# A down product whose sixth chunk is contracted over all 128 rows

## The chip, the cores and the metric

The kernel runs on one NeuronCore of one Trainium2 chip. The metric is the device time of one execution in microseconds. Engines are named as in the profile: PE (TensorE matmuls), PEld (TensorE weight loads), DVE (VectorE), ACT (ScalarE), POOL (GpSimd), SP (SyncE, which issues the DMAs).

## The reference

The program is one transformer-like block on x of shape (4, 2048, 256) in fp32: two kinds of attention without a softmax, each followed by the same feed-forward network, all with a layer norm ahead and a residual sum behind.

```python
x = x + attn_a(layernorm(x))    # projections, exponentials, a weight per head
x = x + ffn(layernorm(x))
x = x + attn_b(layernorm(x))    # products over the 4 batch rows of a token, two gates
x = x + ffn(layernorm(x))

def fp4_linear(x, w):                       # both operands rounded blockwise to a 4-bit grid
    return einsum('bsk,nk->bsn', fp4(x), fp4(w))

def ffn(x):                                 # w_gate, w_up: (704, 256); w_down: (256, 704)
    h = silu(fp4_linear(x, w_gate)) * fp4_linear(x, w_up)
    return fp4_linear(h, w_down)            # the down product
```

`fp4` scales each block of 16 numbers by its largest magnitude and rounds to eight magnitudes. The inner width of 704 matters here: it is 5.5 times 128.

## The kernel before, in words

The 2048 token positions are cut into 16 groups of 128; a group holds the 4 batch rows of its positions, so it is 4 tiles of 128 tokens (`S = 4`, `NJ = 16`). Every group goes through attention a, the first network, attention b and the second network. In a network each of the 4 tiles goes through `ffn_tile`, so there are 16 × 4 × 2 = 128 calls.

One call of `ffn_tile` does this:

1. PE multiplies the tile by both halves of the gate and up weights, 352 columns each (L1190). ACT takes the silu (L1211), DVE multiplies (L1222).
2. DVE, ACT and POOL round the 704 columns to the grid (`quantize`: L340, L1024, L345, L351, L359, L360, L1051).
3. PE transposes the rounded tile in six chunks of 128 columns (L1245), and ACT copies them from PSUM into `hqT`, of shape 128 × 6 × 128 (L1257).
4. PE forms the down product: six matmuls that accumulate in one PSUM bank, chunk i of `hqT` against chunk i of the weights `wdT`, of shape 128 × 6 × 256 (L1270). All operands are fp32, and each matmul stands in the profile as two records.
5. DVE adds the result to the tokens (L301 or L1302).

The chunks start at the columns

```python
HC = [i * 128 for i in range(5)] + [FF - 128]      # 0, 128, 256, 384, 512, 576
```

The sixth starts at 576, not 640, so that it too is a whole 128 × 128 transpose. Its first 64 columns are those that the fifth chunk already covers. So in the kernel before, the sixth matmul uses only rows 64 to 127 of both operands:

```python
rows = slice(P // 2 if i == 5 else 0, P)
```

`wdT` is filled once, near the start: `w_down` is rounded in two pieces, transposed in the same six chunks (L683), and copied from PSUM by ACT in four pieces (L692), which carry the tokens `("wd", 0)` to `("wd", 3)`. Pieces 1 and 3 hold chunks 3 to 5.

The order of the work is not left to the engines. The class `Plan` collects all operations with an engine, an estimated duration, a rank, and the tokens that they read and write, and plays them through in a list scheduler: an engine that is free takes the ready operation with the lowest rank, under the limits of the buffers' pools. The instructions are then issued in that order, and each engine works through its own queue in order. Waits between engines follow from the tiles' contents. A down product has rank `at + 19` and the estimate 2.95 us there.

Of the kernel before, what the change touches and what calls it, by code (L numbers as in the profile page):

```python
# [17 lines left out]
P = 128  # L18
# [4 lines left out]
FF = 704  # L23
HF = FF // 2
FB = FF // BLK

HC = [i * 128 for i in range(5)] + [FF - 128]
LN_EPS = 1e-5
# [8 lines left out]
def blocks(ap, n=BLK):  # L37
    return ap.rearrange("p (g e) -> p g e", e=n)
# [16 lines left out]
class Plan:  # L55
# [23 lines left out]
    def op(self, engine, us, rank, fn, reads=(), writes=(), port=False, table=None, land=0.0, spare=None):  # L79


        i = len(self.ops)
        after = set()
        for t in reads:
            if t in self.last:
                after.add(self.last[t])
        for t in writes:
            after.update(self.readers.get(t, ()))
            if t in self.last:
                after.add(self.last[t])  # L90
        for t in reads:
            self.readers.setdefault(t, []).append(i)
        for t in writes:
            self.last[t] = i
            self.readers[t] = []
        bufs = list(dict.fromkeys(t[0] for t in (*reads, *writes) if isinstance(t[0], Buf)))
        for b in bufs:
            b.users += 1
        self.ops.append(
            dict(engine=engine, us=us, rank=rank, fn=fn, bufs=bufs, port=port, table=table,  # L100
                 land=land, spare=spare or {}, then=[], left=len(after), at=0.0)
        )
        for a in sorted(after):
            self.ops[a]["then"].append(i)
# [108 lines left out]
def kernel(  # L213
# [29 lines left out]
    nc = tc.nc  # L243
# [10 lines left out]
    def one(shape, name, pool=wp, dtype=F32):  # L254
        return pool.tile(shape, dtype, tag=name, name=name)
# [19 lines left out]
    wdT = one([P, 6, D], "wdT")  # L275
# [89 lines left out]
    def tiles(name, n, shape, pool, dtype=F32):  # L365
        made = [one(shape, f"{name}{i}", pool, dtype) for i in range(n)]
        plan.pool(name, made)
        return made
# [6 lines left out]
    floored = tiles("xn", 1, [P, S * D // BLK, BLK + 1], fp)  # L375
    floored += tiles("h", 3, [P, FB, BLK + 1], fp)
    tiles("qax", 2, [P, S * D], fp)
# [4 lines left out]
    tiles("qm", 2, [P, FF], fp, BF16)  # L382
    tiles("sh", 5, [P, 3, FB], fp)
    tiles("hqT", 2, [P, 6, P], fp)
# [14 lines left out]
    def first_pass():  # L399
        op = plan.op  # L400
# [164 lines left out]
        def quantize(at, load, p, n):  # L565
            raw, a, m, w = (plan.buf(t) for t in ("hqT", "qa", "qm", "sh"))
            g = n // BLK

            def ap(b):
                whole = b.ap if len(b.ap.shape) == 2 else b.ap.rearrange("p c n -> p (c n)")  # L570
                return whole[:p, :n]

            def sc(i):
                return w.ap[:p, i, :g]

            op("SP", 0.7, at - 8, lambda: load(ap(raw)), (), [(raw, 0)], land=3.0)
            op(
                "DVE",
                0.9 + n / 1000.0,
                at,  # L580
                lambda: scales(ap(raw), sc(0), sc(1), sc(2)),
                [(raw, 0)],
                [(w, 0)],
            )
            op(
                "DVE",
                0.15 + n / 1000.0,
                at + 1,
                lambda: over_scales(ap(a), blocks(ap(raw)), sc(2)),
                [(raw, 0), (w, 0)],  # L590
                [(a, 0)],
                port=True,
            )
            op(
                "ACT",
                0.2 + n / 1200.0,
                at + 2,
                lambda: to_steps(ap(m), ap(a)),
                [(a, 0)],
                [(m, 0)],  # L600
            )
            op(
                "DVE",
                0.3 + n / 500.0,
                at + 3,
                lambda: to_grid(ap(a), ap(a), ap(m)),
                [(m, 0)],
                [(a, 0)],
                port=True,
            )  # L610
            op(
                "POOL",
                0.2 + n / 550.0,
                at + 5,
                lambda: nc.gpsimd.tensor_mul(
                    blocks(ap(a)), blocks(ap(a)), over_blocks(sc(1))
                ),
                [(w, 0)],
                [(a, 0)],
                port=True,  # L620
            )
            return a
# [10 lines left out]
        for t, (w, wT) in enumerate(((w_gate, wgT), (w_up, wuT))):  # L633
            for i in range(4):
# [13 lines left out]
                def turn(a=a, tp=tp):  # L648
                    for c in range(KC):
                        for t in range(2):  # L650
                            nc.tensor.transpose(
                                tp.ap[:, (2 * c + t) * R : (2 * c + t + 1) * R],
                                a.ap[:R, t * D + c * P : t * D + (c + 1) * P],
                                ident[:R, :R],
                            )
# [13 lines left out]
        for i in range(2):  # L669
            at = 32.0 + 2.0 * i  # L670
            a = quantize(
                at,
                lambda dst, i=i: nc.sync.dma_start(dst, w_down[i * P : (i + 1) * P, :]),
                P,
                FF,
            )
            for h in range(2):
                tp = plan.buf("bank")

                def turn(a=a, tp=tp, h=h):  # L680
                    for c in range(3):
                        at = HC[3 * h + c]
                        nc.tensor.transpose(  # L683
                            tp.ap[:, c * P : (c + 1) * P], a.ap[:, at : at + P], ident
                        )

                op("PE", 0.5, at + 8, turn, [(a, 0)], [(tp, 0)])
                op(
                    "ACT",
                    0.45,  # L690
                    at + 9,
                    lambda tp=tp, h=h, i=i: nc.scalar.copy(  # L692
                        wdT[:, 3 * h : 3 * h + 3, i * P : (i + 1) * P],
                        tp.ap[:, : 3 * P].rearrange("p (c n) -> p c n", c=3),
                    ),
                    [(tp, 0)],
                    [("wd", 2 * i + h)],
                )


        op(
# [222 lines left out]
        op("DVE", 1.4, FIRST, join_biases, [(GROW, "m"), ("rn", 0)], [("ssq", 0), ("bvz z", 0), ("lb", 0)])  # L924

    first_pass()


# [4 lines left out]
    def group(j):  # L933
# [4 lines left out]
        def op(engine, us, at, fn, reads=(), writes=(), **kw):  # L938
            plan.op(engine, us, base + at, fn, reads, writes, **kw)
# [241 lines left out]
        def ffn_tile(at, k, s, xqT):  # L1181
            h, qa, qm, sh = (plan.buf(p) for p in ("h", "qa", "qm", "sh"))
            for half in range(2):
# [3 lines left out]
                def hidden(g=g, u=u, cols=cols):  # L1187
                    for bank, w in ((g, wgT), (u, wuT)):
# [33 lines left out]
                    lambda u=u, sil=sil, half=half: nc.vector.tensor_mul(  # L1222
                        h.ap[:, half * FB // 2 : (half + 1) * FB // 2, :BLK],
                        blocks(sil.ap),
# [14 lines left out]
            hqT = plan.buf("hqT")  # L1239
# [25 lines left out]

            def down():
                for i in range(6):

                    rows = slice(P // 2 if i == 5 else 0, P)
                    nc.tensor.matmul(  # L1270
                        o.ap[:, :D],
                        hqT.ap[rows, i, :],
                        wdT[rows, i, :],
                        start=(i == 0),
                        stop=(i == 5),
                    )
# [3 lines left out]
                2.95,  # L1280
                at + 19,
                down,
                [(hqT, 0), (hqT, 4)] + [("wd", i) for i in range(4)],
                [(o, 0)],
# [308 lines left out]
```

## Time and profile before

| | |
|---|---|
| median of 3 runs | 1665.7 us (1664.18 to 1666.67) |
| the profiled execution's own time | 1663.5 us |
| its span, from the first to the last instruction | 1661.7 us |
| mean granted clock of TensorE | 0.985 |
| PE busy | 1575.4 us (95%) |
| PEld busy | 1058.1 us (64%) |
| DVE busy | 1476.0 us (89%) |
| ACT busy | 808.0 us (49%) |
| POOL busy | 705.7 us (42%) |
| DMA | 27.68 MB, mean 17 GB/s |

A group in the profile stands by line, engine, operation and tiles: out<-in, the number of records, busy time and mean duration of one, then the idle time just before them and what ended it. A form like 64*128 64x256 is rows and columns of the weights in the array, then rows and columns of what streams through. PE records overlap: [...] a weight load can lie under the matmul ahead of it. The ends of matmuls are modelled, their starts are measured. "issue" is time in which the engine waited for nothing that the profile shows.

### The profile page before, as it was taken

To read this page: it belongs to the slowest core of one execution; us is meant where nothing else is said; L and a number is where in the kernel's file an instruction comes from. 1 tells how busy PE (TensorE), PEld (TensorE's weight loads), DVE (VectorE), ACT (ScalarE), POOL (GpSimd) and SP (SyncE) were. 2 spreads that over 40 slices of the span, in tenths; PEclk is the share of its full clock that TensorE was granted. 3 is DMA by queue.
4 is the path that set the end of the run, shared out by engine and by line. 5 is a ranking of instruction groups with operands and counts; after the bars stand their busy time and mean duration, and the time that the engine had idled before them with its cause. 6 is when DMAs were issued, how large, how long until landed. Compare 5 with 4: busy or idle time off the path is not lost.

```text
span 1661.7 us, 18801 instructions
## 1 busy us (share of the span) xinstructions
PE 1575.4 (95%) x6364; PEld 1058.1 (64%) x6364; DVE 1476.0 (89%) x2310; ACT 808.0 (49%) x1738; POOL 705.7 (42%) x739
## 2 busy tenths in 40 slices
PE   7888999999999999999999999999999999889798
PEld 6635656666666676666666666666666666556575
DVE  8988898999898989999997998989999888899874
ACT  5545456463544354545544564553744534353342
POOL 5334346434535343443543443344634424543531
PEclk9989999999999999999999999999999999999899
DMA  8200000000000000000000000000000000000000
GB/s 258 69 9 1 0 1 0 4 7 23 4 20 7 20 7 20 7 20 4 4 23 4 20 4 23 4 4 7 7 7 4 4 7 4 4 7 4 10 16 20
DMA packets 28872, 27.68 MB, mean 17 GB/s; under 512 B 3432, under 2 KB 28520, under 8 KB 28776
## 3 DMA queue, kind: packets, MB, share of 16 engines
q1 hardware_dynamic: 28776, 26.49, 5.1%
q8 instruction: 50, 0.82, 0.2%
q14 instruction: 46, 0.38, 0.1%
HBM read 18.09 MB, written 8.39 MB: 16 GB/s over the span
## 4 chain that ended last, share of the span: by engine, by line
PE 53%; DVE 33%; ACT 4%; POOL 4%; issue 4%; DMA 1%; POOLq 0%; SPq 0%; DVEq 0%; ACTq 0%
PE bank L1190 22%; PE bank L1270 14%; PE bank L981 11%; PE bank L1245 3%; DVE qa L345 3%; DVE qa L359 3%; DVE qa L360 3%; PE bank L958 2%; DVE tok L1497 2%; DVE h L1222 2%; DVE sh L340 2%; DVE pp L1496 2%; DVE x L301 1%; DVE sc L1382 1%; DVE qax L345 1%
## 5 line engine op out<-in xcount | busy, mean ns | idle before, releaser
L1051 POOL TENSOR_TENSOR qa<-qa,sh 128x704 f32<-128x704 f32 x128 | 193.1, 1510 | 461.3 <-DVE qa L360 361.0
L1270 PE MATMUL bank<-wdT,hqT 128*128 128x256 f32 (+1 forms) x1536 | 383.6, 393 | 4.6 <-ACT hqT L1257 3.9
L1190 PE MATMUL bank<-wgT,turned 128*128 128x352 f32 x1024 | 355.2, 470 | 17.0 <-DVE h L1222 12.7
L1190 PE MATMUL bank<-wuT,turned 128*128 128x352 f32 x1024 | 345.6, 460 | 0.4 <-DVE h L1222 0.4
L1270 PEld LDWEIGHTS bank<-wdT,hqT 128*128 128x128 f32 (+1 forms) x1536 | 277.5, 191 | 97.3 <-issue 48.9
L1190 PEld LDWEIGHTS bank<-wuT,turned 128*128 128x128 f32 x1024 | 195.3, 191 | 110.3 <-issue 1.9
L1190 PEld LDWEIGHTS bank<-wgT,turned 128*128 128x128 f32 x1024 | 183.8, 192 | 119.1 <-issue 26.0
L1211 ACT ACTIVATE sil<-bank 128x352 f32<-128x352 f32 x256 | 116.7, 459 | 167.3 <-PE bank L1190 120.5
L1222 DVE TENSOR_TENSOR h<-sil,bank 128x352 f32<-128x352 f32 x256 | 127.9, 508 | 53.8 <-PE bank L1190 46.7
L351 ACT ACTIVATE qm<-qa 128x704 bf16<-128x704 f32 (+1 forms) x138 | 107.6, 781 | 133.7 <-DVE qa L345 128.8
L1257 ACT COPY hqT<-bank 128x512 f32<-128x512 f32 (+1 forms) x256 | 111.0, 479 | 93.7 <-PE bank L1245 93.4
L359 DVE SCALAR_TENSOR_TENSOR qa<-qm,qa 128x704 f32<-128x704 bf16 (+1 forms) x138 | 129.5, 938 | 13.8 <-ACT qm L351 13.8
L360 DVE SCALAR_TENSOR_TENSOR qa<-qm,qa 128x704 f32<-128x704 bf16 (+1 forms) x138 | 137.2, 994 | 4.8
L1478 POOL TENSOR_TENSOR pp<-vg,sc 128x1024 f32<-128x1024 f32 x64 | 132.8, 2089 | 9.1 <-DVE fac L1415 6.0
L345 DVE SCALAR_TENSOR_TENSOR qa<-sh,h 128x704 f32<-128x704 f32 x128 | 131.4, 1031 | 1.9 <-PE bank L1245 0.6
L981 PE MATMUL bank<-wvz,turned 128*128 128x512 f32 x256 | 122.4, 616 | 5.7 <-DVE vz L1079 3.6
L981 PE MATMUL bank<-wqkB,turned 128*128 128x512 f32 x256 | 121.7, 598 | 3.0 <-ACT turned L965 2.6
L965 ACT COPY turned<-bank 128x512 f32<-128x512 f32 x160 | 87.8, 586 | 73.7 <-PE bank L958 72.5
L340 DVE TENSOR_REDUCE sh<-h 128x44 f32<-128x748 f32 x128 | 118.9, 929 | 3.3
L1245 PE MATMUL bank<-ident,qa 128*128 128x128 f32 x768 | 109.4, 278 | 12.3 <-POOL qa L1051 6.0
L1245 PEld LDWEIGHTS bank<-ident,qa 128*128 128x128 f32 x768 | 88.0, 141 | 46.9 <-issue 20.7
L1051 POOL TENSOR_TENSOR qax<-qax,sx 128x1024 f32<-128x1024 f32 x32 | 65.6, 2053 | 81.7 <-DVE qax L360 75.0
(171 smaller groups left out, 2318.2 us busy)
## 6 DMA issues: line engine op xcount, KB each, us to landing
x<-in_L_attn_a_x_dram SPq DMA_DIRECT2D x24, 512.0 KB, 5.1
out_dram<-x SPq DMA_DIRECT2D x64, 128.0 KB, 1.7
hqT<-in_L_ffn_w_gate_dram SPq DMA_DIRECT2D x4, 176.0 KB
hqT<-in_L_ffn_w_up_dram SPq DMA_DIRECT2D x4, 176.0 KB
hqT<-in_L_ffn_w_down_dram SPq DMA_DIRECT2D x2, 352.0 KB
pp<-in_L_attn_a_Wq_dram SPq DMA_DIRECT2D x2, 256.0 KB
pp<-in_L_attn_a_Wk_dram SPq DMA_DIRECT2D x2, 256.0 KB, 5.9
wvz<-in_L_attn_a_Wv_dram SPq DMA_DIRECT2D x1, 256.0 KB
```

What stands on the lines that cost most here:

```text
L340: nc.vector.tensor_reduce(amax, src, AX.X, ALU.max, apply_absolute_value=True)
L345: nc.vector.scalar_tensor_tensor(blocks(a), over_blocks(rs), -6.0 * BELOW, src, ALU.mult, ALU.mult)
L359: nc.vector.scalar_tensor_tensor(a, m, FLOOR, a, ALU.max, ALU.add)
L360: nc.vector.scalar_tensor_tensor(dst, m, FLOOR, a, ALU.max, ALU.subtract)
L981: nc.tensor.matmul(bank.ap[:, :n], lhs.ap[:, c, s * P : (s + 1) * P], w[:, c, :], start=(c == 0), stop=(c == KC - 1),)
L1051: lambda: nc.gpsimd.tensor_mul(blocks(a.ap), blocks(a.ap), over_blocks(q.ap[:, 1, :])),
L1190: nc.tensor.matmul(bank.ap[:, :HF], xqT.ap[:, c, s * P : (s + 1) * P], w[:, c, cols], start=(c == 0), stop=(c == KC - 1),)
L1211: lambda g=g, sil=sil: nc.scalar.activation(sil.ap, g.ap[:, :HF], AF.Silu),
L1222: lambda u=u, sil=sil, half=half: nc.vector.tensor_mul(h.ap[:, half * FB // 2 : (half + 1) * FB // 2, :BLK], blocks(sil.ap), blocks(u.ap[: ...
L1245: nc.tensor.transpose(bank.ap[:, (i - i0) * P : (i - i0 + 1) * P], qa.ap[:, HC[i] : HC[i] + P], ident,)
L1270: nc.tensor.matmul(o.ap[:, :D], hqT.ap[rows, i, :], wdT[rows, i, :], start=(i == 0), stop=(i == 5),)
L1478: nc.gpsimd.tensor_mul(pv.ap.rearrange("p t (n e) -> p t n e", e=HD), vg.ap[:, :, :D].rearrange("p t (n e) -> p t n e", e=HD), over_blocks ...
```

## The change

The sixth matmul takes all 128 rows of `hqT` and `wdT`, like the other five. So that the 64 columns that the fifth chunk covers are not counted twice, the first 64 rows of the sixth weight chunk are set to zero, once, by a memset on POOL. It writes over what ACT copied there and carries the tokens of pieces 1 and 3, so it comes after these two copies and before the first down product.

```diff
@@ after the copies of w_down into wdT
+        op(
+            "POOL",
+            0.3,
+            40.0,
+            lambda: nc.gpsimd.memset(wdT[: P // 2, 5, :], 0.0),
+            (),
+            [("wd", 1), ("wd", 3)],
+        )
@@ ffn_tile
             def down():
                 for i in range(6):
-
-                    rows = slice(P // 2 if i == 5 else 0, P)
                     nc.tensor.matmul(
                         o.ap[:, :D],
-                        hqT.ap[rows, i, :],
-                        wdT[rows, i, :],
+                        hqT.ap[:, i, :],
+                        wdT[:, i, :],
                         start=(i == 0),
                         stop=(i == 5),
                     )
```

The estimate of 2.95 us for the down product is left as it was. Lines of the kernel behind the insertion move by up to nine numbers (the down product from L1270 to L1277).

## Prediction

> **What bounds the kernel now.** I read the page's busy shares first, then the chain, then the PE groups by form, and last the PE timeline around one down product.
>
> ```profile
> PE 1575.4 (95%) x6364; PEld 1058.1 (64%) x6364; DVE 1476.0 (89%) x2310; ACT 808.0 (49%) x1738; POOL 705.7 (42%) x739
> PE   7888999999999999999999999999999999889798
> PEclk9989999999999999999999999999999999999899
> PE 53%; DVE 33%; ACT 4%; POOL 4%; issue 4%; DMA 1%; POOLq 0%; SPq 0%; DVEq 0%; ACTq 0%
> PE bank L1190 22%; PE bank L1270 14%; PE bank L981 11%; PE bank L1245 3%; DVE qa L345 3%; DVE qa L359 3%; DVE qa L360 3%; PE bank L958 2%; DVE tok L1497 2%; DVE h L1222 2%; DVE sh L340 2%; DVE pp L1496 2%; DVE x L301 1%; DVE sc L1382 1%; DVE qax L345 1%
> ```
>
> PE is nearly full from the fifth slice on, at a granted clock of almost 1. VectorE is close behind at 89%. The chain that ends last runs over PE for 53% of the span and over VectorE for 33%, so PE is the first bound but not the only one. The edited line, L1270, holds 14% of the span on that chain by itself.
>
> The groups by form split the down product into its five full chunks and its sixth (each fp32 product leaves two records, so 1280 + 256 records are 128 downs of six products):
>
> ```profile
> L1270 PE MATMUL bank<-wdT,hqT 128*128 128x256 f32 x1280 | 304.8, 386 | 4.6 <-ACT hqT L1257 3.9 <-DVE vz L1079 0.4 <-DVE x L1302 0.2
> L1270 PE MATMUL bank<-wdT,hqT 64*128 64x256 f32 x256 | 89.1, 428 | 0.0
> L1270 PEld LDWEIGHTS bank<-wdT,hqT 64*128 64x128 f32 x256 | 37.7, 184 | 42.8 <-issue 42.8
> ```
>
> Half the rows give a longer matmul record, 428 ns against 386, and 42.8 us of idle weight loader in front of the 64-row loads, for which no engine is named. These are not yet costs, since matmul records overlap and their ends are modelled. Starts are measured, so I take costs from the timeline (start, length, group), first around a down, then around another product of 256 columns with 128 rows throughout:
>
> ```profile
> 1599.09 1.35 PE L1190 MATMUL bank<-wuT,turned 128*128 128x352 f32 x4
> 1600.27 1.04 PE L958 MATMUL bank<-ident,qax 128*128 128x128 f32 x8
> 1601.14 2.95 PE L1270 MATMUL bank<-wdT,hqT 128*128 128x256 f32 x12
> 1604.02 1.45 PE L1190 MATMUL bank<-wgT,turned 128*128 128x352 f32 x4
> 1605.31 1.35 PE L1190 MATMUL bank<-wuT,turned 128*128 128x352 f32 x4
> ...
> 250.55 1.46 PE L981 MATMUL bank<-woB,turned 128*128 128x256 f32 x6
> 251.84 1.35 PE L1190 MATMUL bank<-wgT,turned 128*128 128x352 f32 x4
> 253.03 1.35 PE L1190 MATMUL bank<-wuT,turned 128*128 128x352 f32 x4
> ```
>
> **The change, part by part.**
>
> *The sixth chunk's matmuls.* The control: six records of 256 columns take 251.84 − 250.55 = 1.29 us, 0.216 each, and the next four of 352 columns take 1.19. Around the down, twelve records take 1604.02 − 1601.14 = 2.88 us, where 12 × 0.216 is 2.59, and the following four take 1.29 in place of 1.18 (1600.27 − 1599.09). The excess is 0.29 + 0.10 = 0.39 us. Start to start in the trace, it falls in four places, with almost the same values in all 128 downs: +93 ns into the first 64-row record, +104 between the two of them, +88 to the next 128-row record, and +105 behind that one (+56 where it is a transpose, whose load is shorter). Each is a weight load that waits for the stream ahead instead of lying under it. What follows a down is a product of 256 to 512 columns 77 times, a transpose 50 times, nothing once: 77 × 0.39 + 50 × 0.34 + about 0.6 for the last (its clock is lower) = 47.6 us of PE time.
>
> *What stays in its place.* No 128-row sixth chunk is in the trace. From below: it has as many columns as chunks 0 to 4, so not under 0.216 us a record; from above: it could keep all of the 0.39. The nearest rows are those same five chunks, whose loads all lie under the matmul ahead, and the woB product, behind which a 352-column block loses nothing. Transposes of 88 rows (L651) also run into 128-row ones at the normal cadence, so fewer rows alone do not bring the stall. I take 0 remaining.
>
> [...] 128-row loads run under 128-row matmuls, and the half-height load is the one exposed. I follow the trace.
>
> *Who gains.* Downs on the chain: 14% × 1661.7 = 233 us, and the chain shows each as a piece of 2.79 us, so 83 of 128. Their saving is 83 × 0.385 = 32 us. With the other durations as they are, the span cannot fall below this chain's new length, 1661.7 − 32 = 1630; the saving of the other 45 downs, some 16 us, turns into PE waits. Is there room for the 32? Where the chain stays on PE, VectorE must have idle time to give up. Windows over such stretches (length, PE, PEld, DVE, ACT, POOL busy):
>
> ```profile
> 668.20:745.80 77.60, 77.54 (x321) 53.52 (x322) 70.01 (x113) 42.50 (x94) 36.74 (x38) 1.00 0.04 14
> 806.40:839.40 33.00, 32.98 (x133) 22.29 (x134) 31.78 (x43) 14.34 (x28) 9.75 (x7) 1.00 0.04 11
> 1265.30:1397.10 131.80, 131.78 (x543) 90.97 (x544) 111.53 (x175) 60.46 (x137) 51.05 (x51) 0.99 0.02 6
> 1569.20:1643.90 74.70, 74.68 (x320) 52.92 (x321) 51.66 (x79) 29.51 (x66) 19.92 (x18) 1.00 0.06 18
> ```
>
> They hold 8, 3, 13 and 10 downs on the chain: savings of 3.1, 1.2, 5.0 and 3.9 us against VectorE idle of 7.6, 1.2, 20.3 and 23.0. Room is there, tightly in the second. Not all idle can be given up, as part of it waits for ScalarE (L340 on L334, 22.2 us over the run; L359 on L351, 13.8). I take off 5 us, an estimate of one sixth, as the new waits of PE behind VectorE: 27 us.
>
> *The memset.* One instruction is added on POOL, 64x256 f32; the instruction order on every engine is otherwise unchanged. The nearest memset, 128x128 f32 at the start, took 0.20 us; twice the elements gives at most 0.4. It stands between L1125 and L1051 in POOL's queue and waits for ScalarE's last copies into wdT. Those end at 119.60, POOL is free from 118.46, and L1051 starts only at 124.30, waiting for VectorE: 4.7 us of cover. The first down starts at 148.49, so its added wait on the memset has long been met. Cost 0; uncovered, 0.4 us once. No DMA is added or moved.
>
> *The sum.* The profiled execution took 1663.5 us, 1.8 over its span and 2.2 below the median shown. 1663.5 − 27 = 1636.5; on the scale of the median, 1638.5.
>
> **The rivals.**
>
> *VectorE takes over sooner.* The chain hops between PE and VectorE some thirty times, and a path one hop away may be nearly as long. If only those stretches pass the saving on in which VectorE's idle is over four times it (1265 to 1397, 1569 to 1644, and five shorter ones), 14 us are left: 1651.5. For it: the 806 to 839 stretch, and VectorE's 89%. Against: in the others the cover is two to six times the saving.
>
> *The change does not do what it says.* If the stall belongs to the sixth chunk's place rather than its height, [...] nothing moves: 1665.5. Against: cadence and controls above.
>
> *Slower: the granted clock falls.* [...] The 880 us of PE on the chain make it break even at a loss of 27 / 880 = 3%, that is at 0.97 in the middle; at 0.94 it would cost 54 us and end at 1692. Against: 1.00 or 0.99 stands in just those stretches where PE is fullest; the clock is lower where PE pauses (0.94 from 1450 to 1550 us, with PE busy for 84 of the 100).
>
> **How the numbers follow.** Forecast 0.80, VectorE sooner 0.13, no effect 0.04, clock 0.03. The predicted time is the first's, 1638.5. Low end: the chain's whole 32 us and 1.5 us of spread among the runs, 1632; high end: the first rival with the same spread, 1653. About 0.2%, 3 us, is what a measurement of this kernel can tell from no change. Faster 0.93 (the first two), same 0.04, slower 0.03.
>
> **What would show it.** In the changed profile: no 64*128 form; 1536 down records of 128 rows with a mean near 386; twelve records from a down's start to the next product in 2.59 us; the loader's "issue" idle at L1270 gone (48.9 to a few us); PE busy down by some 45 us and VectorE's share near 90.5%; more PE waits for VectorE than now; POOL's memset near 120 us with L1051 still released by VectorE. The forecast is wrong if the cadence is repaired but the span falls by under 15 us, or if a sixth-chunk load is still exposed.

## The result, and the profile after

The changed kernel took 1645.8 us (median of 4 runs, 1643.0 to 1646.7) against 1664.9 us before, a ratio of 0.988 (95% interval 0.986 to 0.990): 19 us faster. The profiled execution took 1645.8 us, 17.7 under the profiled one of before.

The page after, with the busy line and the chain's two lines:

```profile
PE 1534.1 (93%) x6364; PEld 1078.6 (66%) x6364; DVE 1479.7 (90%) x2310; ACT 807.2 (49%) x1738; POOL 706.1 (43%) x740
...
PE 43%; DVE 41%; POOL 5%; issue 5%; ACT 4%; DMA 0%; POOLq 0%; DVEq 0%; ACTq 0%
PE bank L1199 19%; PE bank L1277 10%; PE bank L990 9%; DVE qa L346 4%; DVE qa L360 3%; DVE qa L361 3%; DVE sh L341 3%; DVE h L1231 3%; PE bank L1254 3%; DVE tok L1504 2%; PE bank L967 2%; DVE pp L1503 2%; DVE sc L1389 2%; DVE x L302 2%; DVE pp L1382 2%
```

PE's busy time fell by 1575.4 − 1534.1 = 41.3 us. Its idle time rose from 86.3 to 109.9 us, so that of the 41.3 us 17.7 are left as the shorter span. On the chain PE and VectorE are now level, 43% and 41%, where they stood at 53% and 33%.

The down product's groups, and after them the PE timeline around one down (start, length, group):

```profile
L1277 PE MATMUL bank<-wdT,hqT 128*128 128x256 f32 x1536 | 354.3, 383 | 6.7 <-ACT hqT L1266 5.7 <-DVE x L1309 0.6 <-DVE vz L1088 0.4
...
L1277 PEld LDWEIGHTS bank<-wdT,hqT 128*128 128x128 f32 x1536 | 289.5, 191 | 58.5 <-ACT hqT L1266 9.8 <-issue 1.2 <-DVE x L1309 0.8
```

```profile
1587.43 2.76 PE L1277 MATMUL bank<-wdT,hqT 128*128 128x256 f32 x12
1590.02 1.35 PE L1199 MATMUL bank<-wgT,turned 128*128 128x352 f32 x4
1591.20 1.05 PE L1199 MATMUL bank<-wuT,turned 128*128 128x352 f32 x3
```

There is one form left. From the start of the down to the next product it is 1590.02 − 1587.43 = 2.59 us, and the four records behind it take 1.18. The idle of the weight loader put down to "issue" at this line is 1.2 us, from 48.9. The stall is gone in full.

### The profile page after: what moved, and what is told of

Same layout as the page of the kernel before. It is cut to its first block, busy times and chain, and to the rows that moved or that the text cites. A ratio compares the mean times of both kernels' runs of the same rounds, so it can differ in the third digit from the quotient of the medians.

```text
span 1644.0 us, 18802 instructions
## 1 busy us (share of the span) xinstructions
PE 1534.1 (93%) x6364; PEld 1078.6 (66%) x6364; DVE 1479.7 (90%) x2310; ACT 807.2 (49%) x1738; POOL 706.1 (43%) x740
## 4 chain that ended last, share of the span: by engine, by line
PE 43%; DVE 41%; POOL 5%; issue 5%; ACT 4%; DMA 0%; POOLq 0%; DVEq 0%; ACTq 0%
PE bank L1199 19%; PE bank L1277 10%; PE bank L990 9%; DVE qa L346 4%; DVE qa L360 3%; DVE qa L361 3%; DVE sh L341 3%; DVE h L1231 3%; PE bank L1254 3%; DVE tok L1504 2%; PE bank L967 2%; DVE pp L1503 2%; DVE sc L1389 2%; DVE x L302 2%; DVE pp L1382 2%
## 5 line engine op out<-in xcount | busy, mean ns | idle before, releaser
L1199 PE MATMUL bank<-wgT,turned 128*128 128x352 f32 x1024 | 350.5, 465 | 20.6 <-DVE h L1231 16.3
L1277 PE MATMUL bank<-wdT,hqT 128*128 128x256 f32 x1536 | 354.3, 383 | 6.7 <-ACT hqT L1266 5.7
L1277 PEld LDWEIGHTS bank<-wdT,hqT 128*128 128x128 f32 x1536 | 289.5, 191 | 58.5 <-ACT hqT L1266 9.8
L346 DVE SCALAR_TENSOR_TENSOR qa<-sh,h 128x704 f32<-128x704 f32 x128 | 134.8, 1058 | 1.9 <-PE bank L1254 0.6
```

What stands on the lines that cost most here:

```text
L346: nc.vector.scalar_tensor_tensor(blocks(a), over_blocks(rs), -6.0 * BELOW, src, ALU.mult, ALU.mult)
L1199: nc.tensor.matmul(bank.ap[:, :HF], xqT.ap[:, c, s * P : (s + 1) * P], w[:, c, cols], start=(c == 0), stop=(c == KC - 1),)
L1277: nc.tensor.matmul(o.ap[:, :D], hqT.ap[:, i, :], wdT[:, i, :], start=(i == 0), stop=(i == 5),)
```

## The experiments

memset_only, low64, low96 and pair64 were each measured once, beside 1664.3 us for the kernel before; the others four times, beside 1665.1 to 1665.3. Of the code, the changed lines alone are shown.

**The memset alone (memset_only).** The kernel before, plus the change's memset; `down` is left as it was.

> The kernel before with the memset alone; the sixth matmul stays at 64 rows, so the zeros are read by nobody. Forecast of the prediction (memset hidden): 1665 us within 3, memset near 119 us, 0.2 to 0.4 us long, ahead of a POOL instruction that is still released by VectorE. Rival (the memset delays POOL or the first down): over 1668.

It took 1663.5 us. POOL's timeline:

```profile
116.73 1.94 POOL L1133 TENSOR_TENSOR vz<-vz,st 128x1024 f32<-128x1024 f32 x1
119.86 0.30 POOL L703 MEMSET wdT<- 64x256 f32 x1 [1.20 <-ACT wdT L692]
124.51 1.98 POOL L1059 TENSOR_TENSOR qax<-qax,sx 128x1024 f32<-128x1024 f32 x1 [4.35 <-DVE qax L360]
```

The memset waits for ScalarE's copy, takes 0.30 us, and POOL then waits another 4.35 us for VectorE. All 128 down products start within 0.4 us of where they start in the kernel before, so the memset costs nothing that can be seen, and the gain is the matmul's alone.

**The other half of the array (low64).**

```diff
-rows = slice(P // 2 if i == 5 else 0, P)
+rows = slice(0, P // 2 if i == 5 else P)
```

> The sixth matmul on rows 0 to 63 in place of 64 to 127 (the last 64 columns of the inner width are left out of the sum, and 64 others are counted twice). If the stall belongs to the height (a change between half-height and full-height matmuls): twelve records from the start of a down to the next product in 2.88 us as before, time about 1665. If it belongs to the upper half of the array: 2.59 us and about 1646.

**96 rows (low96).**

```diff
-rows = slice(P // 2 if i == 5 else 0, P)
+rows = slice(0, 96 if i == 5 else P)
```

> The sixth matmul on rows 0 to 95 (sums over 32 of the last columns left out, 64 columns counted twice). If only a height of 64 rows or fewer makes the array change over, and 96 rows count as full: 2.59 us for twelve records and about 1646. If every height under 128 brings the stall: 2.88 us and about 1665; the 88-row transposes near the start, which had none, speak against that.

**Two half-height matmuls in a row (pair64).**

```diff
-rows = slice(P // 2 if i == 5 else 0, P)
+rows = slice(P // 2 if i >= 4 else 0, P)
```

> The fifth and the sixth matmul both on rows 64 to 127 (the first half of the fifth chunk is left out of the sum). If the cost is paid at the change of height, twice per down however many half-height matmuls stand in a row: 2.88 us for twelve records as before, about 1665. If each half-height matmul has its loads exposed: another 0.2 to 0.39 us per down, so 3.08 to 3.27 us, and 1682 to 1715.

The partial-height group of each, in the order low64, low96, pair64:

```profile
L1270 PE MATMUL bank<-wdT,hqT 64*128 64x256 f32 x256 | 89.2, 428 | 0.0
```

```profile
L1270 PE MATMUL bank<-wdT,hqT 96*128 96x256 f32 x256 | 76.4, 379 | 0.0
```

```profile
L1270 PE MATMUL bank<-wdT,hqT 64*128 64x256 f32 x512 | 144.7, 403 | 0.0
```

The times were 1665.5 us for low64, 1643.6 for low96 and 1664.5 for pair64. From the start of a down to the next product it is 2.88 us in low64 and pair64 and 2.59 in low96 (medians of the traces). So the lower half stalls like the upper one: place is not the cause. 96 rows run like 128, with a mean of 379 ns and the changed kernel's time: a partial height by itself is not the cause either. A second half-height matmul beside the first adds nothing to the time, and the group's mean falls from 428 to 403 ns, as it does if only the first record of four is drawn out by an exposed load (before, the first of a down's two took 480 ns and the second 376; (480 + 3 × 376) / 4 = 402): the price is paid at the change of height and not by each half-height matmul. Of the 0.39 us for a change there and one back, the starts show about 0.09 us of waiting and 0.10 of exposed load each way: in the trace of before the first 64-row load starts 308 ns behind the start of the matmul ahead (median), where the cadence is 216, and the second 64-row record 320 ns behind the first. What the array does at such a change is not shown; the runs show the price, and that 96 rows do not pay it.

**Twice as many changes of height (twice64).**

```diff
-rows = slice(P // 2 if i == 5 else 0, P)
+rows = slice(P // 2 if i in (2, 5) else 0, P)
```

> The third matmul too on rows 64 to 127 (half of the third chunk left out), so four changes of height per down in place of two. Theory of the chain (PE's saving was lost since VectorE's path is nearly as long, while added PE time cannot be hidden on a chain that is already the longest): at least 83 x 0.39 = 32 us more than before, so 1697 to 1714, and 3.27 us for twelve records. Rival (each change of height is worth the same everywhere, 19 us per 128 downs): 1684.

It took 1707.6 us, ratio 1.025 (1.024 to 1.027): 42 us slower than before, over the chain's minimum of 32. Not all of it is the height: behind the 109th down its trace has 34.5 us at half the granted clock, that of before 28.1. But at the 109th down it is already 34.4 us behind. Down to next product is 3.27 us in its PE timeline:

```profile
1566.59 3.34 PE L1270 MATMUL bank<-wdT,hqT 128*128 128x256 f32 x12
1569.86 1.45 PE L1190 MATMUL bank<-wgT,turned 128*128 128x352 f32 x4
```

The same PE time costs 42 us when it is added and returns 19 when it is taken away.

**Half of the stalls, one way and the other (half64, half64b).** The memset is in; the sixth matmul stays at 64 rows in two of the four tiles of a group.

```diff
-rows = slice(P // 2 if i == 5 else 0, P)
+rows = slice(P // 2 if i == 5 and s % 2 else 0, P)        # half64
+rows = slice(P // 2 if i == 5 and not s % 2 else 0, P)    # half64b
```

> The memset is in; the sixth matmul stays at 64 rows in the tiles s = 1 and 3 and takes 128 rows in s = 0 and 2, so half of the stalls are gone (64 x 0.38 = 24 us of PE time). If savings run out as VectorE takes over: more than half of the gain already, 11 to 14 us under before, 1651 to 1654. If the passing share is the same throughout: 9.5 us, 1655.5.

> The memset is in; the sixth matmul stays at 64 rows in the tiles s = 0 and 2 and takes 128 rows in s = 1 and 3, the other half of the stalls. With s = 0 and 2 repaired alone the time fell by only 6 us, so the thought that the first savings pass best has failed. If what passes depends on where in the order a stall lies: s = 1 and 3 are worth the other 13 us, 1652. If the first savings pass worst, whichever they are, since two paths have to be shortened: again 5 to 8 us, 1657 to 1660.

half64 took 1659.1 us, ratio 0.996 (0.995 to 0.998): 6 us for half of the PE time, where both theories had wanted more. half64b took 1653.3 us, ratio 0.993 (0.991 to 0.995): 12 us. This looks as if what passes depended on where in the order a stall lies, and the two together give 18 of the 19. But the clock was not the same. The windows from 1434 to 1570 us, of before, half64 and half64b (the granted clock is the third number from the end):

```profile
1434.00:1570.00 136.00, 112.09 (x425) 74.42 (x424) 122.53 (x166) 52.11 (x109) 64.98 (x53) 0.92 0.02 6
1434.00:1570.00 136.00, 114.65 (x429) 78.41 (x430) 117.83 (x164) 52.00 (x109) 59.00 (x48) 0.87 0.02 6
1434.00:1570.00 136.00, 115.28 (x460) 80.00 (x460) 120.71 (x173) 56.55 (x120) 57.69 (x48) 0.93 0.02 7
```

In the traces, at the 109th down, ahead of this stretch, half64 led the kernel before by 6.2 us, half64b by 9.3 and the changed kernel by 12.1; at the 128th the leads were 4.8, 12.2 and 16.3. So more than half of the difference between the two halves arose where half64 had the lower clock, and all four of its runs had a lower mean clock (0.979 to 0.981, against 0.983 to 0.984 for the kernel before beside it). Why is not known. How much depends on the place of a stall therefore stays open, and the thought that the first savings pass best is not refuted: up to the 109th down the leads of the two halves sum to 15.5 us, more than the changed kernel's 12.1 or the 14.4 of low96.

**Less work on VectorE (lite_before, lite_after).** In both kernels the reciprocals of h's block maxima are left out (the tile holds ones, written once).

```diff
-        nc.vector.reciprocal(rs, amax)
+        if src.shape[1] != FB:
+            nc.vector.reciprocal(rs, amax)
 ...      # the memsets that fill the tiles with ones
```

> The kernel before without the reciprocal of the block maxima of h (128 VectorE instructions of 0.43 us, 55 us of VectorE time; a constant 1 stands in its place). It is the base for the next run. If PE is the first bound of before: far less than 55 us gained, about 1640 to 1655. If VectorE bounds it: 1620 or less.

> The changed kernel without the same reciprocals. If the 28 us that the sixth chunk's saving lost went to VectorE's path: the gain over the run without reciprocals on the kernel before rises from 19 to 30 or more of the 47 us. If the loss lies with ScalarE, POOL or the order of the queues: the gain stays at 15 to 22.

1648.8 us (ratio to before 0.990, 0.989 to 0.991) and 1628.2 us (0.978, 0.976 to 0.980). The change is worth 20.5 us on this base: a miss for the theory that VectorE's path took the rest, at this size of relief. VectorE's busy time had only fallen from 1476.0 to 1431.3 us, 87% of that span.

**Much less work on VectorE (deep_before, deep_after).** The second rounding pass of h is left out as well.

```diff
-        nc.vector.scalar_tensor_tensor(dst, m, FLOOR, a, ALU.max, ALU.subtract)
+        if not short:      # short: the passes over h
+            nc.vector.scalar_tensor_tensor(dst, m, FLOOR, a, ALU.max, ALU.subtract)
```

> The kernel before with much less on VectorE: the reciprocals of the block maxima of h are left out, and the second rounding pass of h too (another 128 instructions, 1.0 us each); the values are no longer those of the network. Base for the next run. PE's own path, with its stalls of 47 us, should bound it nearly alone: 1600 to 1640.

> The changed kernel with the same two things left out. If VectorE's path took the lost 28 us: with some 150 us less on VectorE the gain over its own base is 35 us or more of the 47. If the loss lies with waits for ScalarE and POOL or with the fixed order of the queues, whatever VectorE's load: 15 to 25. The first try, with 45 us less on VectorE, gave 20.5 and left that open.

1621.4 us (0.974, 0.972 to 0.975) and 1585.7 us (0.952, 0.950 to 0.953). The change is now worth 35.6 us, of the 47.6 that it saves on PE. Busy line and chain of deep_before:

```profile
PE 1561.8 (96%) x6364; PEld 1057.4 (65%) x6364; DVE 1306.8 (81%) x2054; ACT 809.0 (50%) x1738; POOL 681.5 (42%) x744
...
PE 86%; DVE 9%; ACT 2%; POOL 1%; issue 1%; DMA 0%; POOLq 0%; DVEq 0%; ACTq 0%
PE bank L1193 36%; PE bank L1273 20%; PE bank L984 19%; PE bank L1248 5%; PE bank L961 4%; DVE half_moments L539 2%; DVE moments L540 1%; DVE qa L346 1%; ACT xn L334 0%; DVE x L301 0%; DVE qax L362 0%; DVE qa L360 0%; DVE sx L340 0%; DVE qax L360 0%; ACT hqT L1260 0%
```

With VectorE at 81%, PE holds 86% of the chain. Down products hold 20% × 1619.9 = 324 us of it, which is 116 of 128 at 2.79 us, so the chain's bound is 45 us and 80% of it arrived. Before, the bound was 32 and 17.7 arrived, 55%. So VectorE's load held back more than half of the lost time: 28 of the 47.6 us of PE time did not arrive before, 12 do not here. Since 45 us of relief raised the gain from 19 to 20.5 us and 170 us raised it to 35.6, the effect is not proportional to VectorE's work; why the first part brought so little stays open.

**Another estimate for the planner (plan26).** The changed kernel, reordered.

```diff
         op(
             "PE",
-            2.95,
+            2.6,
             at + 19,
             down,
```

> The changed kernel with the planner's estimate of the down product at 2.6 us in place of 2.95, near to the 2.59 that the timeline now shows; this reorders a large part of every queue. If the loss comes from an order that was planned for the slow down product: 1640 or less. If it comes from VectorE's own path, or one order is as good as another: 1642 to 1650, and a worse order by chance is possible too.

1636.6 us (1635.5 to 1639.2), ratio to before 0.983 (0.982 to 0.985), 9 us under the changed kernel, and the fastest of the kernels that leave nothing out. PE's busy time is as in the changed kernel, and its idle time is 103 us in place of 110:

```profile
PE 1531.2 (94%) x6364; PEld 1081.5 (66%) x6364; DVE 1480.7 (91%) x2310; ACT 805.4 (49%) x1738; POOL 702.7 (43%) x740
...
PE 51%; DVE 31%; POOL 6%; ACT 5%; issue 4%; DMA 2%; POOLq 0%; SPq 0%; DVEq 0%; ACTq 0%
```

This shows that some of the lost time was within reach. It does not show that the better estimate is the reason: nearly every queue is in a new order, and only one new order was tried.

## Why the prediction was right, point by point

The forecast was 1638.5 us, 27 us faster; measured were 1645.8 and 19. The range held, and the causes that it names held. But the number lies a little nearer to the rival of an earlier VectorE (1651.5) than to the forecast: the loss to VectorE was nearly three times what the forecast took off. (1665.7 − 27 is 1638.7; the 0.2 changes nothing.)

- *The stall and its price.* Right: 0.39 us a down before, none of it after, with twelve records in 2.59 us. low64, low96 and pair64 show the cause as a change between half and full height, which the trace of before could not tell from the place. The loads of the transposes, where the stall behind a down was shorter, took 141 ns.
- *Nothing stays.* Right. The loader's "issue" idle of 1.2 us leaves no room for exposed loads at full height: the 128-row loads of the down start 2 ns behind the start of the matmul ahead (median), before and after the change. The length of a load is not the price: 184 ns at 64 rows and 192 at 128 before, 191 after.
- *The memset.* Right: 0.30 us under a wait of POOL that goes on for 4.35 us behind it.
- *83 of 128 downs on the chain, at most 32 us.* Held as a bound: 17.7 us came. From the other side twice64 fits it as a minimum for added work, 42 against 32, or 34.4 up to the 109th down.
- *"I take off 5 us, an estimate of one sixth."* This is the term that was mis-sized: 32 − 17.7 = 14.3 us were lost. The check behind it was too weak. It compared the saving of a stretch with VectorE's idle in the same stretch, but idle VectorE time between two waits is no sign that the path through VectorE is short. The starts of the down products in the two traces show where little came through. The 55th began at 794.7 us before and 784.3 after, 10.4 us ahead; the 85th at 1162.5 and 1153.0, 9.5 ahead. Thirty downs, 30 × 0.37 = 11 us of PE time, and no gain. Part of this is the clock: in the trace of after alone it stood at half for 3.4 us at 1144 us (0.66 over the window from 1143 to 1148), some 1.7 us of PE's work. In low96, with the same rhythm and without that dip, the lead grew by 2.3 us over the same downs. So about 2 of the 11 us came. The windows between these points, of before and of after (length, PE, PEld, DVE busy first):

```profile
794.70:1162.50 367.80, 359.43 (x1433) 236.83 (x1432) 333.46 (x486) 179.88 (x383) 153.59 (x148) 1.00 0.03 10
```

```profile
784.30:1153.00 368.70, 351.76 (x1430) 242.01 (x1431) 337.52 (x487) 180.21 (x385) 152.37 (x148) 1.00 0.03 10
```

PE is busy 7.7 us less in as long a stretch, and idle for 16.9 us in place of 8.4. VectorE works through the same instructions at 91 to 92% and 4 us slower. The chain of these windows, summed by engine, lies on PE for 58% before and 31% after, and on VectorE for 35% and 54%. In the prediction's terms, its first rival (VectorE takes over sooner) held in this stretch, over a fifth of the span, and the forecast in others: between the 115th down (1532.2 us before) and the 127th (1645.0) the lead grew by 3.6 us, of the 12 × 0.37 = 4.4 that PE was spared.
- *New waits.* Right in kind. The waits for VectorE's h in front of PE grew from 13.0 to 16.6 us, and VectorE waited for PE less. Before, and then after:

```profile
PE bank L1190 <- DVE h L1222: 13.0, 9, 5.7
DVE h L1222 <- PE bank L1190: 46.7, 35, 3.0
DVE sx L340 <- ACT xn L334: 22.2, 15, 2.8
DVE x L1302 <- PE bank L1270: 16.7, 15, 8.4
DVE qa L359 <- ACT qm L351: 13.8, 21, 1.5
DVE x L301 <- PE bank L1270: 13.4, 17, 2.2
...
PE bank L1199 <- DVE h L1231: 16.6, 12, 5.6
DVE h L1231 <- PE bank L1199: 36.3, 29, 2.8
DVE sx L341 <- ACT xn L335: 26.0, 16, 2.7
DVE qa L360 <- ACT qm L352: 13.1, 19, 1.4
DVE x L1309 <- PE bank L1277: 10.3, 8, 6.8
DVE x L302 <- PE bank L1277: 8.1, 9, 2.0
```

VectorE's three waits for PE here are 22 us shorter together; the two for ScalarE did not shrink together (36.0 before, 39.1 after). That is the part of VectorE's idle which a faster PE cannot use.
- *The clock.* Its mean stayed at 0.985; the slower case did not come up.

## What to carry to other kernels

In a stream of full-height matmuls, one over 64 rows can cost more than it saves (0.39 us a down here; fewer than 64 were not tried): look at the starts behind it, not at its own duration, and pad it with zeros where the operands are there. The share of a line on the chain of waits bounds from above what its repair can bring in the same order of work, and from below what a slowdown costs. How much of the bound arrives depends on the second engine: here 17.7 of 32 us came with VectorE at 89%, 35.6 of 45 with it at 81%. After a repair, try another order too: the one that was tried here brought 9 us more.

## What was not expected of the hardware

A height of 96 rows cost nothing (379 ns a record, 1643.6 us in all), while 64 rows cost 0.39 us a down on either half of the array. And VectorE's first pass over h took 1058 ns on average after the change, 1031 before (L346, then L345), 3.4 us over the run for the same work; what slows it was not tried. Short dips of the granted clock, to half for 3.4 or 6.8 us in the traces of before and after, fell partly in other places from run to run (at 1144 us after the change, at 438 us in low64, at 828 us in twice64, at none of these before; the mean clocks were 0.985, 0.984, 0.983 and 0.985) and can look like an effect of the change; compare the clock of a stretch before comparing its time.
